# One rounding buffer, asked for once, for the second batch's four token blocks of a quantised GLU kernel

## The chip, the core and the metric

The kernel runs on one core of one Trainium2 chip. The core has five engines that run side by side, each with its own instruction queue that it works off in order: TensorE (PE, with its weight loads shown apart as PEld), VectorE (DVE), ScalarE (ACT), GpSimd (POOL) and SyncE (SP), which issues nearly all of this kernel's DMA transfers. The metric is the time of one execution on the device in microseconds (us), as the median of several runs.

## The reference

For each of four batches, 1024 tokens of width 512 are normalised, scaled by a gain that comes from a condition vector, multiplied by an up-projection of 4096 rows, gated, rounded to 8 bits per token, and multiplied by a down-projection whose weights are rounded to -1, 0 or 1:

```python
scale = cond @ norm_w.T + 1.0
ms = jnp.mean(x * x, axis=-1, keepdims=True)
h = x * (scale[:, None, :] * jax.lax.rsqrt(ms + EPS))
u = h @ up_w.T
val, gate = jnp.split(u, 2, axis=-1)
h = val * jax.nn.gelu(gate, approximate=False)
hq = act_quant(h)          # per token: round(h * 127 / max|h|), scaled back
wq = weight_quant(down_w)  # round(w / mean|w|) in -1, 0, 1, scaled back
return hq @ wq.T + x
```

## The kernel before

**Arithmetic.** The up-projection needs more digits than one f16 number holds, so each f32 operand is kept as two f16 numbers, a high part (the value rounded to f16) and a low part (the rest). One product of a 256-wide piece then takes six matmuls: high by low, low by high and high by high, for two blocks of 128 (`TERMS`). Weights and tokens are both cut into two halves, and the four block products of a 2x2 block multiplication are made from seven (`C_ALL = 7`), with sums and differences of the halves as operands.

**Stages.** Batch b has 16 slots, one for each block of 128 hidden columns; slot g = 16b + j makes the gate and the value of block j for all 1024 tokens of the batch. The first batch is made in another way while the weights are still being prepared: its blocks 0 to 11 by plain products (`half_gate`, `half_value`), its blocks 12 to 15 by slots. The order of everything in this stage is written out by hand in a long string, `FIRST_BATCH`, in which each word is a step: `slot.14.5` is the sixth step of slot 14, `t_high.3.2` is step `high` of token block 3, part 2. Each engine takes its steps in the order of the string. The steps of a slot have numbers: 0 is the first product, 1 its copy into bank B, 2 the fourth product (its copy is 3), 4 the fifth product, which adds to the first one's bank, 5 its copy to t2 (line 820), 6 the second product, 8 the third, 10 the gate product, 13 the value product, which adds to the bank that step 5 has copied.

**The second batch's tokens.** In the same stage the tokens of batch 1 are made ready, in four blocks a = 0 to 3 of 2 x 128 tokens (class `Tokens`). For each block: load; square and root; scale by the gain; four sums of halves; then `high` (ACT casts f32 to f16, line 665), `low` (DVE subtracts, line 669) and `turn` (SP issues a DMA transpose into the big tile `R`, line 673). These last three come in three parts: part 0 is operands 0 and 1 (written `nx[:, 0:2]`), part 1 is operand 2 (`nx[:, 2:3]`), part 2 is operands 3 to 6 (`nx[:, 3:7]`). The tile `nx` that holds the high and low parts before the transpose is the rounding buffer of this document. It is asked for by `place` from a pool with one buffer (`tag="nx", bufs=1`). A tile asked for from such a pool may be written first when every access to the tile before it in that place is over, whatever region that access touched.

**The order around block 3.** Blocks 2 and 3 follow each other in the buffer. SP turns block 2 as part 2, part 0, part 1. Between part 0 and part 1 stand, in SP's queue, a weight transpose, two transposes of the last weight rows and spills, and the first load of a piece of the down-projection (`d_fetch`, line 546). On ACT the casts `t_high.3.2` and `t_high.3.0` stand ahead of `slot.14.3`, a small gain, and `slot.14.5`. After them ACT casts the last weight rows of block 15 (`s_high.15.1`, line 453), POOL subtracts (`s_low.15.1`, line 457), and SP turns them (`s_turn.15.1`, line 475), followed by block 3's part 0 and part 2. Slots 14 and 15 and then batch 1's slots 16, 17 and on are what PE has next. SP's transfers use eight completion semaphores, DMAHW0 to DMAHW7, one after the other; each transfer waits for the one that used its semaphore last.

Of the kernel before, what the change touches and what calls it, by code (L numbers as in the profile page):

```python
# [51 lines left out]
def glu_quant_kernel(  # L52
# [108 lines left out]
    def h_slots(g, n=1):  # L161
        s = g % NSLOT
        return H[:, s : s + n]
# [414 lines left out]
    class Tokens:  # L578
# [69 lines left out]
            ]  # L648

        def place(self):  # L650
            if self.nx_at is None:
                self.nx = wpool.tile(
                    [P, C_ALL, 2, HALF], F16, name=f"nx_{self.b}_{self.a}", tag="nx", bufs=1
                )
            else:
                v = h_slots(self.nx_at, 2).bitcast(F16).rearrange("p s h t -> p (s h t)")
                self.nx = v[:, : C_ALL * 2 * HALF].rearrange(
                    "p (c l d) -> p c l d", c=C_ALL, l=2
                )
# [366 lines left out]
    class Pair:  # L1026
# [12 lines left out]
        def sum1(self, place):  # L1039
            self.s[1] = place.bitcast(BF16)  # L1040
            DVE.tensor_tensor(self.s[1], self.part(1, 0), self.part(1, 1), ALU.add)
# [237 lines left out]
    toks, ams, made = {}, {}, {}  # L1279
# [247 lines left out]
    for b in range(1, B):  # L1527
# [23 lines left out]
        if b + 1 < B:  # L1551
            sc = []
            steps[3, "z"] = [(lambda b=b, sc=sc: sc.append(cond_load_scale(b + 1)), (0, 0))]
            steps[5, "z"] = [(lambda b=b, sc=sc: cond_bring(b + 1, sc[0]), (0.4, 0))]
            p0 = b * NJ + 12
            plan = [
                (None, p0, ((6, "z"), (7, "x"), (7, "y"), (9, "y"), (10, "x"), (10, "z"))),
                (p0 + 4, None, ((9, "y"), (10, "x"), (10, "y"), (11, "y"), (12, "x"), (12, "x"))),
                (None, None, ((10, "y"), (11, "x"), (11, "y"), (13, "x"), (13, "y"), (13, "z"))),
                (p0 + 2, p0 + 4, ((9, "z"), (12, "x"), (12, "y"), (14, "x"), (14, "y"), (14, "z"))),  # L1560
            ]
            for a, (at, nx_at, places) in enumerate(plan):
                def make(a=a, at=at, nx_at=nx_at, b=b):
                    toks[a] = Tokens(b + 1, a, at, nx_at)
                    toks[a].load()
                fs = [
                    make,
                    lambda a=a: toks[a].norm(),
                    lambda a=a, sc=sc: toks[a].scale_and_sum(sc[0]),
                    lambda a=a: toks[a].high(),  # L1570
                    lambda a=a: toks[a].low(DVE),
                    lambda a=a: toks[a].turn(),
                ]
                costs = ((0, 0), (0, 1.6), (0, 1.5), (0, 2.1), (2.6, 0), (0, 0))
                for place, f, c in zip(places, fs, costs):
                    steps.setdefault(place, []).append((f, c))
# [250 lines left out]
```

## Time and profile before

| | |
|---|---|
| Median of 3 runs | 728.83 us (728.76 to 731.47) |
| The profiled execution's own time | 728.52 us |
| Its span, first to last instruction | 726.4 us |
| PE busy | 714.6 us, 98% of the span |
| DVE busy | 589.7 us, 81% |
| ACT busy | 423.0 us, 58% |
| POOL busy | 135.7 us, 19% |
| Granted TensorE clock, mean | 0.995 of full speed |

The span is 2.1 us less than the time of the same execution. Slots and products can be followed in the rows of line 698 (seven-product scheme, six matmuls each) and line 713 (plain). In the profile, a row of a timeline gives the start in us from the span's start, the duration, engine, line, operation and tiles, how often, and in brackets how long the engine stood idle ahead of it and what ended that. SPq is SP's sequencer, so the duration there is the issue of a transfer, not the transfer. A row of waits reads: engine, tile and line that waited, what it waited for, total us, times, longest us. Of overlapping instructions on one engine each has its own start, so a row's start plus duration may lie a little past the next row's start.

### The profile page before, as it was taken

How to read it: one execution, taken by the hardware profiler on the slowest of the kernel's cores; microseconds unless marked ns; L12 is line 12 of the kernel's file. 1: busy time of each engine (PE TensorE's matmuls, PEld its weight loads, DVE VectorE, ACT ScalarE, POOL GpSimd, SP SyncE). 2: the span in 40 equal slices, each digit the busy share in tenths (PEclk: the TensorE clock that was granted, in tenths of full speed). 3: DMA queues.
4: the chain of work that ended last, by engine and by line, in shares of the span. 5: the costliest groups of instructions: out<-in, count | busy, mean ns of one | idle time of the engine just before them, and what ended most of it. 6: DMA issues, size and time to landing. Idle time of an engine off the chain costs nothing.

```text
span 726.4 us, 10223 instructions
## 1 busy us (share of the span) xinstructions
PE 714.6 (98%) x3664; PEld 360.1 (50%) x3664; DVE 589.7 (81%) x880; ACT 423.0 (58%) x703; POOL 135.7 (19%) x143
## 2 busy tenths in 40 slices
PE   8999999996999999999999999999999999999998
PEld 4544444442444446665444445666444444445854
DVE  7898898885898879898688877877679888765896
ACT  6998777664757775544335676544433665333463
POOL 1712323240100033540010030360020000000120
PEclk9999999998999999999999999999999999999999
DMA  6899899997886644976745546865955444444243
GB/s 221 282 268 297 236 232 261 251 214 171 218 197 153 153 110 159 193 184 163 172 102 117 131 101 175 197 153 153 218 103 109 102 103 102 100 93 109 103 156 134
DMA packets 227060, 121.57 MB, mean 167 GB/s; under 512 B 188969, under 2 KB 198461, under 8 KB 227010
## 3 DMA queue, kind: packets, MB, share of 16 engines
q1 hardware_dynamic: 226858, 120.80, 66.6%
q8 instruction: 28, 0.46, 0.3%
q14 instruction: 22, 0.18, 0.1%
q10 hardware_dynamic: 152, 0.13, 0.1%
HBM read 52.71 MB, written 23.09 MB: 104 GB/s over the span
## 4 chain that ended last, share of the span: by engine, by line
PE 96%; ACT 1%; DMA 1%; DVE 1%; issue 0%; SPq 0%; POOL 0%; ACTq 0%
PE A L698 36%; PE E L698 18%; PE po L1062 9%; PE B L698 9%; PE pg L713 8%; PE pv L713 8%; PE po_end L1014 4%; PE pz L1179 1%; DMA R<-nx 1%; PE ptx L1163 1%; DMA R<-s_rows 0%; PE pv L784 0%; PE po_B L1062 0%; PE pg L784 0%; PE pw L382 0%
## 5 line engine op out<-in xcount | busy, mean ns | idle before, releaser
L698 PEld LDWEIGHTS <-SXY 128*128 128x128 f16 x2100 | 205.6, 98 | 241.0 <-issue 0.8
L698 PE MATMUL A<-R,SXY 128*128 128x512 f16 x1146 | 265.1, 379 | 0.0
L698 PE MATMUL E<-R,SXY 128*128 128x512 f16 x582 | 141.4, 379 | 0.0
L833 DVE SCALAR_TENSOR_TENSOR H<-A,sg,t 128x512 f32<-128x512 f32 x52 | 39.0, 750 | 67.5 <-PE A L698 67.3
L985 DVE TENSOR_TENSOR H<-H,am 128x1024 f32<-128x1024 f32 x64 | 76.0, 1213 | 0.0
L844 ACT ACTIVATE t<-t,sg 128x512 f32<-128x512 f32 x52 | 37.5, 720 | 62.8 <-DVE t L841 62.6
L698 PE MATMUL B<-R,SXY 128*128 128x512 f16 x300 | 72.9, 379 | 0.0
L904 DVE TENSOR_REDUCE gm<-H 128x512 f32<-128x1024 f32 x56 | 69.0, 1232 | 1.0
L827 ACT ACTIVATE t<-B,sg 128x512 f32<-128x512 f32 x52 | 35.7, 687 | 37.6 <-PE B L698 37.5
L920 POOL PARTITION_ALL_REDUCE am<-R x8 | 14.3, 1793 | 231.4 <-DVE R L906 231.4
L713 PEld LDWEIGHTS <-SXY 128*128 128x128 f16 x342 | 33.4, 98 | 40.3 <-DVE SXY L424 0.4
L1062 PE MATMUL po<-wd,R 128*128 128x256 fp8e4 x416 | 52.4, 273 | 0.0
L820 ACT COPY t<-A 128x512 f32<-128x512 f32 x52 | 30.2, 580 | 37.9 <-PE A L698 37.5
L813 ACT COPY v<-E 128x512 f32<-128x512 f32 x52 | 30.4, 585 | 31.8 <-PE E L698 31.4
L1062 PEld LDWEIGHTS <-R 128*128 128x128 bf16 (+1 forms) x448 | 43.8, 98 | 8.9
L805 ACT COPY B<-A 128x512 f32<-128x512 f32 x52 | 29.7, 572 | 31.6 <-PE A L698 30.8
L853 DVE SCALAR_TENSOR_TENSOR H<-v,sg,t 128x512 f32<-128x512 f32 x52 | 41.0, 789 | 7.1 <-ACT t L844 7.1
L850 DVE TENSOR_TENSOR v<-A,v 128x512 f32<-128x512 f32 x52 | 35.6, 685 | 10.3 <-PE A L698 8.7
L993 ACT ACTIVATE H<-H 128x1024 f32<-128x1024 f32 x38 | 39.9, 1050 | 5.2 <-DVE H L985 5.2
L713 PE MATMUL pg<-R,SXY 128*128 128x512 f16 x180 | 41.3, 379 | 0.0
L906 DVE TENSOR_TENSOR R<-R,gm 128x512 f32<-128x512 f32 x56 | 40.1, 716 | 1.1
L997 ACT ACTIVATE R<-H 128x1024 bf16<-128x1024 f32 x38 | 40.1, 1056 | 1.0
(237 smaller groups left out, 951.1 us busy)
## 6 DMA issues: line engine op xcount, KB each, us to landing
SXY<-s_dram SPq DMA_DIRECT2D x46, 256.0 KB, 3.2
H<-in_L_cond_up_w_dram SPq DMA_DIRECT2D x13, 512.0 KB, 4.8
SXY<-s_dram SPq DMA_DIRECT2D x46, 128.0 KB, 3.3
s_dram<-SXY SPq DMA_DIRECT2D x15, 384.0 KB, 5.1
xr<-in_x_dram SPq DMA_DIRECT2D x19, 256.0 KB, 2.9
out_dram<-xr SPq DMA_DIRECT2D x19, 256.0 KB, 2.5
H<-in_x_dram SPq DMA_DIRECT2D x8, 512.0 KB, 7.8
R<-in_L_cond_down_w_dram SPq DMA_DIRECT2D x8, 512.0 KB, 7.0
```

The lines of the kernel that those rows point to most:

```text
L698: PE.matmul(o, s[:, w, k, :], operand(g // NJ, c, l, k), start=start and n == 0, stop=stop and n == len(TERMS) - 1, skip_group_check=True,)
L713: PE.matmul(ps, a[k // 2][:, w, k % 2, :], XP[:, l, k, h * TOK : (h + 1) * TOK], start=n == 0, stop=n == len(terms) - 1,)
L827: ACT.activation(self.t1, self.B, AF.Gelu, scale=gain(self.g, 1))
L833: DVE.scalar_tensor_tensor(h_half(self.g, 0), self.A, gain(self.g, 0), self.t1, ALU.mult, ALU.mult)
L844: ACT.activation(self.t2, self.t2, AF.Gelu, scale=gain(self.g, 1))
L853: DVE.scalar_tensor_tensor(h_half(self.g, 1), self.v, gain(self.g, 0), self.t2, ALU.mult, ALU.mult)
L904: DVE.tensor_reduce(gm[0], v, AX.X, ALU.max, apply_absolute_value=True)
L906: return [largest, lambda: DVE.tensor_tensor(m, m, gm[0], ALU.max)]
L985: DVE.tensor_tensor(v, v, r.to_broadcast([P, 2, TOK]), ALU.mult)
L993: ACT.activation(v, v, AF.Copy, bias=MAGIC)
L997: ACT.activation(q, by_tile(v), AF.Copy, bias=-MAGIC)
L1062: PE.matmul(po, w[:, j], m, start=start and j == 0, stop=stop and j == n - 1, skip_group_check=True,)
```

## The change

```diff
         def place(self):
-            if self.nx_at is None:
+            if self.nx_at is None and self.b == 1 and self.a:
+                self.nx = toks[0].nx
+            elif self.nx_at is None:
                 self.nx = wpool.tile(
                     [P, C_ALL, 2, HALF], F16, name=f"nx_{self.b}_{self.a}", tag="nx", bufs=1
                 )
```

Block 0 of batch 1 asks for the buffer as before. Blocks 1, 2 and 3 of batch 1 take the same tile object. The bytes are the same bytes as before, since the pool had one buffer for this tag. What differs is what the framework waits for: a write to a region of a tile that is already held waits for the accesses to that region alone. Batches 2 and 3 are not touched.

No instruction is added, removed or moved: on PE, DVE, ACT, POOL and SP the instructions stand in the same order before and after (lines behind the edit are numbered 2 higher). What changes is the list of semaphores in front of eight casts on ACT and six subtractions on DVE that write the buffer. The place that the prediction speaks of is ACT's, at block 3. Before, ACT from the weight cast of block 15 to the copy of slot 14's fifth product:

```order
L805 COPY B_14_1661<-A_14_1654 128x512 [waits PE_49,Activation_49]
L453 CAST s_rows_15_0_1676<-H_79 128x2x256 [waits DMAHW2_49,DMAHW1_49,DVE_49]
L665 CAST nx_1_3_1683<-xt_1_3_1497 128x4x256 [waits DMAHW2_49,DMAHW0_49,DMAHW3_49,DVE_49,Pool_49]
L665 CAST nx_1_3_1683<-xa_1_3_1496 128x2x256
L813 COPY v_14_1702<-E_14_1666 128x512 [waits DVE_49,PE_49]
L360 ACTIVATE sg_0_104<-sw_103,dx_101 128x4
L820 COPY t2_14_1711<-A_14_1654 128x512 [waits PE_49,Activation_49]
```

The same place after the change:

```order
L807 COPY B_14_1659<-A_14_1652 128x512 [waits PE_49,Activation_49]
L453 CAST s_rows_15_0_1674<-H_79 128x2x256 [waits DMAHW2_49,DMAHW1_49,DVE_49]
L667 CAST nx_1_0_963<-xt_1_3_1495 128x4x256 [waits DMAHW0_49,DVE_49,Pool_49]
L667 CAST nx_1_0_963<-xa_1_3_1494 128x2x256 [waits DMAHW3_49]
L815 COPY v_14_1699<-E_14_1664 128x512 [waits DVE_49,PE_49]
L360 ACTIVATE sg_0_104<-sw_103,dx_101 128x4
L822 COPY t2_14_1708<-A_14_1652 128x512 [waits PE_49,Activation_49]
```

The first cast of block 3 waited for DMAHW0, DMAHW3 and DMAHW2, that is for all three transposes of block 2; now it waits for DMAHW0 alone, which is part 2's transpose, and the second cast waits for DMAHW3, part 0's. The wait for DMAHW2, part 1's, moves to the cast of part 1, some fifteen instructions further on in ACT's queue. The value of the DVE semaphore that the first cast waits for also falls by one, from the last subtraction of block 2 to the last sum of block 3.

SP's transfers from block 2's first transpose on, before the change (the same afterwards but for names); a row that waits for a DMAHW semaphore is also the one that raises it next, and the first row raises DMAHW0:

```order
L673 DMA_TRANSPOSE R<-nx_2_1425 128x16x128 [waits DVE_49]
L475 DMA_TRANSPOSE R<-s_rows_0_1592 128x8x128 [waits DMAHW1_49,DVE_49]
L469 DMA s_dram<-s_rows_0_1592 128x1024 [waits DMAHW2_49]
L673 DMA_TRANSPOSE R<-nx_2_1425 128x8x128 [waits DMAHW3_49]
L406 DMA_TRANSPOSE SXY<-H 128x12x128 [waits DMAHW4_49,DVE_49,PE_49]
L475 DMA_TRANSPOSE R<-s_rows_1_1593 128x8x128 [waits DMAHW5_49,DVE_49]
L469 DMA s_dram<-s_rows_1_1593 128x1024 [waits DMAHW6_49]
L469 DMA s_dram<-s_rows_0_1676 128x1024 [waits DMAHW7_49,Pool_49]
L475 DMA_TRANSPOSE SXY<-s_rows_0_1676 128x8x128 [waits DMAHW0_49]
L546 DMA dn_1713<-in_L_cond_down_w_dram 128x1024 [waits DMAHW1_49,DVE_49]
L673 DMA_TRANSPOSE R<-nx_2_1425 128x4x128 [waits DMAHW2_49]
L546 DMA dn_1725<-in_L_cond_down_w_dram 128x1024 [waits DMAHW3_49,DVE_49]
```

Part 1's transpose (the row of 4x128) stands ten transfers behind part 2's and seven behind part 0's. Blocks 1 and 2 get the same kind of edit on their casts: block 1's first cast no longer waits for part 1 of block 0, and block 2's first cast waits for part 0 of block 1 where it waited for all three parts.

## Prediction

> **What bounds the kernel now.** I read the page first, then the waits of the first 240 us, then the chain and the timelines around the one long wait.
>
> ```profile
> PE   8999999996999999999999999999999999999998
> ```
>
> The row is PE's busy share in 40 slices of 18.2 us. PE is full almost everywhere, so time can be won only where PE stands still: one slice, the tenth (163 to 182 us), shows a 6, and behind it come thirty full ones. Whatever PE loses in the tenth slice, the whole rest of the kernel starts later by that much.
>
> ```profile
> ACT nx L665 <- DMA R<-nx: 8.3, 1, 8.3
> DVE nx L669 <- ACT nx L665: 7.5, 1, 7.5
> PE A L698 <- ACT t L820: 5.8, 1, 5.8
> ```
>
> These three single waits are one event. ACT stands 8.3 us in front of a cast into the rounding buffer, until a transpose out of that buffer has landed; DVE then waits for the cast; and PE waits 5.8 us for a copy that stands behind the cast in ACT's queue. The chain that ended last goes through it:
>
> ```profile
> 164.88 4.49 DMA R<-nx
> ...
> 169.55 0.07 ACT nx L665
> ```
>
> The transpose issued at 164.88 landed at 169.37. On PE it looks like this:
>
> ```profile
> 163.75 1.46 PE L698 MATMUL A<-wd,R 128*128 128x512 f16 x6
> 165.04 1.46 PE L698 MATMUL E<-R,SXY 128*128 128x512 f16 x6
> 172.32 2.72 PE L698 MATMUL A<-wd,R 128*128 128x512 f16 x6 [5.82 <-ACT t L820]
> 174.84 1.75 PE L698 MATMUL A<-R,SXY 128*128 128x512 f16 x6
> 176.42 1.46 PE L698 MATMUL E<-wd,SXY 128*128 128x512 f16 x6
> ...
> 184.19 1.46 PE L698 MATMUL A<-R 128*128 128x512 f16 x6
> 185.49 1.46 PE L698 MATMUL E<-R 128*128 128x512 f16 x6
> ```
>
> A product of six matmuls comes every 1.295 us (163.75 to 165.04). Without a wait the value product of slot 14 would start at 166.34 and the one that stands at 176.42 at 165.04 + 3 x 1.295 = 168.93. It comes 7.49 us late. Of that, 172.32 - 166.34 = 5.98 us are standstill, and 1.51 us are two products that ran slowly after it. The granted clock (the number ahead of the DMA share) says why:
>
> ```profile
> 166.00:168.00 2.00, 0.50 (x3) 0.11 (x2) 0.00 (x0) 0.00 (x0) 0.00 (x0) 1.00 0.92 234
> 168.00:170.00 2.00, 0.00 (x0) 0.00 (x0) 0.00 (x0) 0.45 (x1) 0.00 (x0) 0.65 0.40 77
> 170.00:172.00 2.00, 0.00 (x0) 0.00 (x0) 1.37 (x2) 2.00 (x5) 0.00 (x0) 0.50 0.01 4
> 172.00:174.00 2.00, 1.68 (x5) 0.57 (x5) 2.00 (x5) 0.84 (x2) 1.08 (x1) 0.50 0.41 125
> 174.00:176.00 2.00, 2.00 (x8) 0.80 (x7) 1.51 (x4) 1.30 (x2) 0.07 (x1) 0.65 0.73 208
> ```
>
> It falls to 0.50 during the standstill and stays there for the first products after it.
>
> **The change, part by part.** Nothing is added, removed or moved; only waits differ. Blocks 1 and 2 first: their casts lose waits too, but of the whole line 665 the table of waits has one entry, the 8.3 us above. A wait that cost nothing gives nothing back: 0.
>
> Block 3's first cast. It waited for all of block 2's transposes, and the last of them, part 1, is the one issued at 164.88. Now it needs part 2's transpose, DVE's and POOL's sums, and ACT free.
>
> ```profile
> 160.64 0.62 ACT L453 CAST s_rows<-H 128x512 f16<-128x512 f32 x1
> 169.55 1.04 ACT L665 CAST nx<-xt 128x1024 f16<-128x1024 f32 x1 [8.29 <-DMA R<-nx]
> 170.50 0.61 ACT L665 CAST nx<-xa 128x512 f16<-128x512 f32 x1
> 171.02 0.58 ACT L813 COPY v<-E 128x512 f32<-128x512 f32 x1
> 171.70 0.57 ACT L820 COPY t<-A 128x512 f32<-128x512 f32 x1
> 172.22 0.62 ACT L453 CAST s_rows<-H 128x512 f16<-128x512 f32 x1
> ```
>
> ```profile
> 160.53 0.41 DVE L634 TENSOR_TENSOR xt<-xa 128x256 f32<-128x256 f32 x1
> 162.36 0.73 DVE L853 SCALAR_TENSOR_TENSOR H<-v,sg,t 128x512 f32<-128x512 f32 x1
> 170.63 1.23 DVE L669 TENSOR_TENSOR nx<-xt,nx 128x1024 f16<-128x1024 f32 x1 [7.54 <-ACT nx L665]
> ...
> 172.71 0.74 DVE L833 SCALAR_TENSOR_TENSOR H<-A,sg,t 128x512 f32<-128x512 f32 x1
> ```
>
> ```profile
> 158.07 0.72 POOL L634 TENSOR_TENSOR xt<-xa,xt 128x256 f32<-128x256 f32 x1
> 172.92 1.15 POOL L457 TENSOR_TENSOR s_rows<-H,s_rows 128x512 f16<-128x512 f32 x1 [10.42 <-ACT s_rows L453]
> ```
>
> ```profile
> 150.05 2.54 SPq L673 DMA_TRANSPOSE R<-nx  x1
> 156.64 1.29 SPq L673 DMA_TRANSPOSE R<-nx  x1
> 164.88 1.20 SPq L673 DMA_TRANSPOSE R<-nx  x1
> 171.88 0.34 SPq L546 DMA_DIRECT2D dn<-in_L_cond_down_w_dram  x1
> 174.10 1.24 SPq L475 DMA_TRANSPOSE SXY<-s_rows  x1
> 175.43 1.30 SPq L673 DMA_TRANSPOSE R<-nx  x1
> 177.40 1.68 SPq L673 DMA_TRANSPOSE R<-nx  x1
> ```
>
> ```profile
> DMA to landing us min/median/max: 5.2/5.8/7.0
> dn<-in_L_cond_down_w_dram SPq DMA_DIRECT2D x3, 512.0 KB, 4.5
> ```
>
> The first three SP rows are block 2's parts 2, 0 and 1; the last two are block 3's parts 0 and 2; the last fence has the landing times of line 673's transposes, as far as the profile gives them, and of the down-projection loads. Step by step:
>
> - The cast of part 2: POOL's sums end at 158.79, DVE's at 160.94, the transpose at 150.05 + 7.0 = 157.05 at the latest, ACT's cast before it at 161.26. It starts at 161.3, not 169.55, and ends at 162.3.
> - The cast of part 0: its transpose has landed by 156.64 + 7.0 = 163.64 at the latest, so it ends between 162.9 and 164.25.
> - The copy of v needs DVE's row of 162.36, which ends at 163.09: over by 164.83 at the latest, the small gain by 165.1.
> - The copy t (line 820) needs slot 14's fifth product, whose row ends at 163.75 + 1.46 = 165.21. It then takes 0.57 us: 165.8. PE wants it at 166.34. The standstill is gone with 0.5 us to spare, and with it the slow clock.
>
> So PE is 7.49 us earlier from the slot 15 products on. The other engines are free when that is asked of them: DVE's subtractions of block 3 come right after 163.1, or after the second cast, instead of at 170.63. From there to the end of the read that frees slot 13's bank are 173.45 - 170.63 = 2.82 us, which puts that end near 166 us, ahead of 167.63, when slot 15's first product wants the bank.
>
> What is late next is the queue of SP, which gains less than PE. The load at 171.88 stood 6.1 us for DVE's subtraction; that is now over at about 164.3, so the load goes out when SP is free, 164.88 + 1.20 = 166.1: 5.8 us earlier. The weight transpose at 174.10 waits for POOL, POOL for ACT's cast at 172.22, and that cast now follows the t copy at 165.8: ACT ends at 166.4, POOL 1.15 us later at 167.6, so 6.5 us earlier. Block 3's transposes follow at 168.9 and 170.9. Batch 1's first product needs part 0 at 184.19 - 7.49 = 176.7, its fourth needs part 2 at 178.0. With the longest landing seen they are there at 175.9 and 177.9. Both hold, the second by 0.1 us at the worst landing and by 1.3 us at the median. From there on PE drives SP and DVE, and all move together to the end.
>
> Sum: 728.52 us of the profiled execution - 7.49 = 721.0. The median of the runs is 0.31 us above that execution, which gives 721.3 us. The most the wait itself could return is ACT's 8.3 us, hence 720.5 as the edge below; I take 720.3 with the spread of the runs.
>
> **The rivals.**
>
> *A, the transfers take a part back.* The three transposes and the 512 KB load come 5.8 to 6.5 us earlier, into DMA engines that were 0.92 busy at 166 to 168 and drained only by 170 (0.40, then 0.01). If that backlog must be gone first, the group can start at 169.37 rather than 171.88 and moves by 2.5 us alone. Part 2 of block 3 then lands at 177.40 + 5.8 - 2.5 = 180.7, at worst 181.9, and PE waits 2.7 to 3.9 us for it at 178.0. The gain shrinks to between 4.8 and 3.6 us: 724.0 to 725.2. Against it speaks that the backlog is thin: of the stretch from 168 to 170 it fills 0.40.
> The Trainium skill, "DMA: Bandwidth & Descriptors", section "Queues, rings and completion order", speaks for A: on each DMA engine descriptors are consumed in the order of the ring, and SP owns one ring per engine, so the load that now goes out earlier stands ahead of the transposes that PE needs. By that rule alone the sum would be A's 724.0 to 725.2, if the ring is still full; the row at 168 to 170 says it is 0.40 busy by then, so it bites for part of the way only.
>
> *B, nothing comes of it.* Another wait on ACT stands as late as the one removed, and t is copied at about 171.8 as before: 728.8. For it: a wait for several things is put down to the last, and others may hide behind it. Against it: each of the others is worked out above, and the latest is at 163.64.
>
> *C, slower.* Block 3's part 2 lands so late that PE stands longer than it does now, and the clock falls again. That needs a landing after 185.49, the time at which the fourth product of slot 16 starts today, 14.6 us after its new issue at 170.9, against 7.0 in the longest row. At 2 us beyond that point: 730.8.
>
> **How the numbers follow.** My own case (gain 6 to 8.3 us, 720.3 to 722.8) gets 0.73, since each step of it rests on a row and only the transfers lack one; A gets 0.13, B 0.06, C 0.08 for everything that I don't see. About half a per cent, 3.6 us, is what a measurement of this kernel can tell from no change, so faster means below 725.2: 0.73 + 0.12 of A = 0.85. B and the rest of A make 0.07 for the same, C 0.08 for slower. The range is my case and the nearer part of A: 720.3 to 724.8.
>
> **What would show it.** In the profile after: no row of the cast line waiting on R<-nx for over 1 us; the cast at about 161.3 and t's copy at 165.3; PE's value product at 166.3 with no bracket behind it; a granted clock of 1.00 from 160 to 180; the digit 6 of the tenth slice a 9. If A holds, a new wait of PE stands near 178 us with R<-nx as its releaser. I am wrong if slot 14's value product still waits for the copy of t, or if PE stands still anywhere between 170 and 200 us.

## The result and the profile after

Over eight runs of each kernel on one chip the median falls from 729.37 us (728.34 to 731.47) to 724.18 us (721.33 to 726.84). The ratio is 0.9927 with a 95% interval of 0.9903 to 0.9951. On two other chips the same changed kernel had medians of 721.32 us (ratio 0.9901, 0.9888 to 0.9914) and 721.71 us (0.9911, 0.9895 to 0.9927). The three intervals overlap, and together they reach from a gain of 0.5% to one of 1.1%.

The profiled execution of the changed kernel took 722.66 us, with a span of 720.8 us and a mean granted clock of 1.000 (before 728.52, 726.4 and 0.995). Lines behind the edit are numbered 2 higher: 698 is now 700, 665 is 667, 673 is 675, 820 is 822, 805 is 807. This profile also starts its middle part 0.35 us earlier than that of before (slot 14's fourth product at 164.69 instead of 165.04), so a time read from it is compared with the prediction after adding 0.35.

The row of PE's busy share over 40 slices:

```profile
PE   8999999999899999999999999999999999999998
```

The 6 of the tenth slice is a 9. An 8 stands in the eleventh, 180 to 198 us. The table of waits for the stretch from 100 to 260 us, cut to the rows that matter (engine, tile and line, what was waited for, total us, times, longest):

```profile
ACT dn L550 <- issue: 3.5, 1, 3.5
...
PE B L700 <- ACT B L807: 1.7, 1, 1.7
...
PE A L700 <- ACT t L822: 0.2, 1, 0.2
```

The wait of the cast for R<-nx, 8.3 us before, is not in the table any more, and PE's wait for the copy t has gone from 5.8 to 0.2 us (that 0.2 is at another slot, 184.5 us). In their place stand two others: ACT stands 3.5 us at line 550, where it stood 1.15 us before, and PE 1.7 us for a copy of line 807, a wait that the profile of before does not have. First the place of the edit. ACT's timeline at block 3:

```profile
160.29 0.62 ACT L453 CAST s_rows<-H 128x512 f16<-128x512 f32 x1
160.82 1.04 ACT L667 CAST nx<-xt 128x1024 f16<-128x1024 f32 x1
161.76 0.61 ACT L667 CAST nx<-xa 128x512 f16<-128x512 f32 x1
162.83 0.59 ACT L815 COPY v<-E 128x512 f32<-128x512 f32 x1 [0.45 <-DVE H L855]
...
164.95 0.59 ACT L822 COPY t<-A 128x512 f32<-128x512 f32 x1 [1.34 <-PE A L700]
```

The first cast follows the weight cast without a gap. The copy t no longer stands behind the cast; it waits for PE, whose fifth product it reads. PE's timeline there, and where the new wait is:

```profile
163.40 1.46 PE L700 MATMUL A<-wd,R 128*128 128x512 f16 x6
164.69 1.46 PE L700 MATMUL E<-R,SXY 128*128 128x512 f16 x6
165.99 1.46 PE L700 MATMUL A<-wd,R 128*128 128x512 f16 x6
167.28 1.46 PE L700 MATMUL A<-R,SXY 128*128 128x512 f16 x6
168.58 1.46 PE L700 MATMUL E<-wd,SXY 128*128 128x512 f16 x6
...
187.12 1.46 PE L700 MATMUL E<-R,SXY 128*128 128x512 f16 x6
190.28 1.46 PE L700 MATMUL B<-R,SXY 128*128 128x512 f16 x6 [1.71 <-ACT B L807]
```

From 163.40 to 168.58 a product comes every 1.295 us with no bracket. At 190.28 the second product of slot 17 comes 190.28 - 187.12 - 1.295 = 1.87 us late. The chain that ended last, between 160 and 192 us, tells where that is from (an "issue" row is idle time for which the profile names no releaser):

```profile
177.67 5.54 DMA R<-nx
...
184.48 3.51 issue
187.99 1.15 ACT dn L550
189.14 0.61 ACT t L846
189.75 0.49 ACT B L807
...
190.28 1.46 PE B L700 x6
```

SP's timeline gives the transfers (for SPq the duration is that of the issue). The row L675 at 177.67 turns part 1 of block 3; the next one is the load of the down-projection's piece 3:

```profile
175.54 0.44 SPq L546 DMA_DIRECT2D H<-in_L_cond_down_w_dram  x1
177.67 1.29 SPq L675 DMA_TRANSPOSE R<-nx  x1
183.22 0.34 SPq L546 DMA_DIRECT2D dn<-in_L_cond_down_w_dram  x1
```

And the same three rows of the kernel before:

```profile
180.42 0.45 SPq L546 DMA_DIRECT2D H<-in_L_cond_down_w_dram  x1
185.51 1.20 SPq L673 DMA_TRANSPOSE R<-nx  x1
187.96 0.34 SPq L546 DMA_DIRECT2D dn<-in_L_cond_down_w_dram  x1
```

Then ACT's rounding of piece 3 and its copy into bank B, and the product that reads the copy, all before the change:

```profile
192.91 1.15 ACT L550 ACTIVATE dn<-dn,wsc 128x1024 f32<-128x1024 f32 x1 [1.15 <-issue]
...
194.75 0.57 ACT L805 COPY B<-A 128x512 f32<-128x512 f32 x1
```

```profile
195.84 1.46 PE L698 MATMUL B<-R,SXY 128*128 128x512 f16 x6
```

and the same copy after it:

```profile
189.66 0.57 ACT L807 COPY B<-A 128x512 f32<-128x512 f32 x1
```

Piece 3 is loaded into the rounding buffer's place: in the code, `d_fetch(3)` asks for a tile with the same tag `nx`. So it waits for the transpose of block 3's part 1 to have read the old contents. With the 0.35 us taken off, that transpose is issued 7.49 us earlier than before, as much as PE gained. But the 512 KB load of piece 2 ahead of it (the rows of 180.42 and 175.54) comes only 4.5 us earlier, so the transpose now stands 2.1 us behind that load and not 5.1. The load of piece 3 goes out 5.55 us after the transpose's issue instead of 2.45, and so gains 4.4 us and not 7.5. It is on ACT's queue that this is felt: line 550 rounds piece 3, and behind it stands the copy into bank B that PE's second product waits for. The profile names no releaser for ACT's wait there. That it is the load is read from the code and from the times: ACT begins 4.8 us after the load's issue, and began 4.95 us after it before.

### The profile page after: what moved, and what is told of

The parts are those of the page before. It is cut to its first block, busy times and chain, and to the rows that moved or that the text cites. A ratio compares the mean times of both kernels' runs of the same rounds, so it can differ in the third digit from the quotient of the medians.

```text
span 720.8 us, 10222 instructions
## 1 busy us (share of the span) xinstructions
PE 712.9 (99%) x3664; PEld 359.6 (50%) x3664; DVE 589.5 (82%) x880; ACT 423.2 (59%) x703; POOL 134.7 (19%) x143
## 4 chain that ended last, share of the span: by engine, by line
PE 97%; DMA 1%; ACT 1%; issue 1%; DVE 0%; SPq 0%; DVEq 0%
PE A L700 36%; PE E L700 18%; PE po L1064 9%; PE B L700 9%; PE pg L715 8%; PE pv L715 8%; PE po_end L1016 4%; DMA R<-nx 1%; PE pz L1181 1%; PE ptx L1165 1%; PE pv L786 0%; PE po_B L1064 0%; PE pg L786 0%; PE pw L382 0%; PE po_A L1064 0%
```

## The experiments

The kernels ran in three groups, each on a chip of its own, and each is compared with runs of the kernel before on the same chip. Those had medians of 728.37 us (first four rows), 729.19 us (next four) and 728.49 us (last two).

| run | median us (range) | ratio to before, 95% interval |
|---|---|---|
| block 3 alone | 722.80 (721.49 to 725.05) | 0.9922 (0.9907 to 0.9938) |
| blocks 1 and 2 alone | 728.76 (727.91 to 729.36) | 1.0001 (0.9992 to 1.0010) |
| the change again | 721.32 (720.30 to 722.52) | 0.9901 (0.9888 to 0.9914) |
| part 1 earlier | 720.45 (720.22 to 721.51) | 0.9891 (0.9878 to 0.9904) |
| turn earlier, no shared tile | 722.44 (721.19 to 722.86) | 0.9912 (0.9898 to 0.9925) |
| PE kept busy in the wait | 727.65 (726.86 to 730.52) | 0.9981 (0.9972 to 0.9990) |
| rounding of piece 3 later | 721.25 (720.58 to 721.84) | 0.9898 (0.9884 to 0.9911) |
| small load of piece 2 | 720.71 (719.89 to 720.79) | 0.9888 (0.9875 to 0.9902) |
| the change, third chip | 721.71 (721.26 to 724.73) | 0.9911 (0.9895 to 0.9927) |
| part 1 earlier, third chip | 720.75 (720.48 to 721.01) | 0.9889 (0.9874 to 0.9904) |

### Which block holds the gain

Block 3 alone takes block 2's tile; blocks 1 and 2 ask for their own as before:

```diff
-            if self.nx_at is None:
+            if self.nx_at is None and self.b == 1 and self.a == 3:
+                self.nx = toks[2].nx
+            elif self.nx_at is None:
```

> Only block 3 takes the held buffer (block 2's); blocks 1 and 2 ask for a new one as before. My theory (all of the gain is the 8.3 us wait of block 3's first cast): the same as the full change, 721 to 725 us, no wait of ACT on R<-nx over 1 us, PE's standstill of 5.8 us gone, the granted clock 1.00 from 160 to 180 us. Rival (the gain needs the looser waits of blocks 1 and 2 as well): between 725 and 729 us, with part of the 8.3 us wait left.

The other half, in which block 3 asks for its own:

```diff
-            if self.nx_at is None:
+            if self.nx_at is None and self.b == 1 and self.a in (1, 2):
+                self.nx = toks[0].nx
+            elif self.nx_at is None:
```

> Blocks 1 and 2 take block 0's buffer; block 3 asks for a new one. My theory: as the kernel before, 728.3 to 730 us, with ACT's wait of about 8.3 us on R<-nx and PE's 5.8 us standstill. Rival (blocks 1 and 2 carry part of the gain): below 727 us.

Block 3 alone gave 722.80 us, blocks 1 and 2 alone 728.76 us against 728.37 us of before. The waits of the second run, 100 to 260 us, still hold the old event:

```profile
ACT nx L667 <- DMA R<-nx: 8.1, 1, 8.1
...
PE A L700 <- ACT t L822: 5.6, 1, 5.6
```

So the gain is block 3's, and the waits of blocks 1 and 2 cost nothing, as worked out. Block 3 alone shows the new wait too, and longer, 4.7 us on ACT and 2.8 us on PE. That is 1.1 us more on PE than with the whole change, whose median on the same chip is 1.5 us lower (next section); the two intervals overlap.

### The change again

> The changed kernel once more, on the chip of the other three, since its eight runs went from 721.3 to 726.8 us. My theory (the scatter comes from the new wait: ACT for the down-projection load that stands behind block 3's part 1 in the buffer, 3.5 us on ACT and 1.7 us on PE in the profile of after): PE's wait is again there, between 0.5 and 5 us, and the time is 721 plus about that wait. Rival (the scatter is the chip's, as of any kernel): the kernel before scatters as widely beside it.

It gave 721.32 us, and the same new waits in its profile: 3.5 us on ACT at line 550 and 1.7 us on PE. Its four runs lie within 2.2 us and the seventeen of the kernel before beside it within 1.8 us, so on this chip alone the spread does not tell the two apart.

### The new wait taken away by order

Part 1's cast, subtraction and transpose stand earlier in the written order, so that the transpose is issued ahead of piece 2's load. Nothing else differs from the changed kernel:

```diff
-        slot.13.11 slot.13.12 max.4.0.1 slot.15.0 slot.14.7 slot.14.14 slot.15.1 max.5.0.0 t_turn.3.0
-        slot.15.2 slot.13.15 slot.15.3 s_spill.11.2 slot.15.6 max.5.0.1 t_turn.3.2 max.4.1.0 slot.14.8
+        slot.13.11 slot.13.12 max.4.0.1 slot.15.0 slot.14.7 slot.14.14 slot.15.1 t_high.3.1 max.5.0.0 t_turn.3.0
+        slot.15.2 slot.13.15 t_low.3.1 slot.15.3 s_spill.11.2 slot.15.6 max.5.0.1 t_turn.3.2 t_turn.3.1 max.4.1.0 slot.14.8
...
-        t_high.3.1 slot.14.12 slot.15.14 d_sign.1 t_low.3.1 t_turn.3.1 slot.14.15 max.6.0.0 d_fetch.3
+        slot.14.12 slot.15.14 d_sign.1 slot.14.15 max.6.0.0 d_fetch.3
```

> The change, and block 3's part 1 (cast, subtraction, transpose) moved ahead by about 6 us: the cast behind slot 15's first copy, the transpose right behind part 2's. Thereby the buffer is free, and the down-projection load that reuses it goes out, about 4 us earlier. My theory (the 1.9 us that are missing from the forecast 7.5 are this load's wait): no wait of PE over 0.5 us from 160 to 240 us, time 720.0 to 721.5 us, and little scatter. Rival (the transfers as a whole are too slow once the standstill is gone): the wait shows up again at another transfer, and the time stays at 722 to 725 us.

It gave 720.45 us, 7.9 us below before. SP's timeline (the two transposes of block 3's parts 2 and 1 share a row):

```profile
171.81 3.68 SPq L675 DMA_TRANSPOSE R<-nx  x2
...
177.71 0.44 SPq L546 DMA_DIRECT2D dn<-in_L_cond_down_w_dram  x1
```

Piece 3's load goes out at 177.71, 5.5 us earlier than in the changed kernel, and PE's products run through the place of the new wait:

```profile
186.90 1.46 PE L700 MATMUL E<-R,SXY 128*128 128x512 f16 x6
188.19 1.46 PE L700 MATMUL B<-R,SXY 128*128 128x512 f16 x6
```

The interval of this run overlaps that of the change again, so the times alone do not prove the 0.9 us between their medians; the two profiled executions differ by 722.52 - 720.57 = 1.95 us, and the 1.87 us at the second product are gone.

### The wait shortened without the shared tile

The kernel before, with block 2's last transpose moved up on SP, ahead of two transfers of weight rows and the first load. No tile is shared, so block 3's cast still waits for it, only for less long:

```diff
-        s_high.15.0 s_low.15.0 t_low.2.1 max.4.0.0 t_high.3.2 slot.14.6 t_high.3.0 slot.12.15 s_spill.15.0
+        s_high.15.0 s_low.15.0 t_low.2.1 t_turn.2.1 max.4.0.0 t_high.3.2 slot.14.6 t_high.3.0 slot.12.15 s_spill.15.0
...
-        t_turn.2.1 t_low.3.0 slot.13.10 slot.13.9 d_fetch.1 s_high.15.1 s_low.15.1 s_turn.15.1 slot.14.13
+        t_low.3.0 slot.13.10 slot.13.9 d_fetch.1 s_high.15.1 s_low.15.1 s_turn.15.1 slot.14.13
```

> The kernel before, every block with a new buffer as before, but the transpose of block 2's part 1 moved ahead of three transfers in SP's queue (a spill, a weight transpose, a down-projection load), so that it can go out about 3.4 us earlier, at 161.5 instead of 164.9. My theory (that transpose's landing is what ACT's cast waits for, and PE loses what ACT waits plus the slow clock): it lands near 166, ACT waits 4 to 5.5 us instead of 8.3, PE stands 2 to 3 us instead of 5.8, the clock stays at 1.00, and the time is 723.5 to 725.5 us. Rival (the wait has another releaser behind it): ACT waits over 7 us, time 728 to 729.5 us.

It gave 722.44 us. Its chain, then ACT's and PE's timelines:

```profile
161.83 2.45 DMA R<-nx
```

```profile
164.38 1.04 ACT L665 CAST nx<-xt 128x1024 f16<-128x1024 f32 x1 [2.88 <-DMA R<-nx]
```

```profile
167.15 1.46 PE L698 MATMUL A<-wd,R 128*128 128x512 f16 x6 [0.42 <-ACT t L820]
```

The transpose was issued 3.05 us earlier and landed after 2.45 instead of 4.49 us, so the cast came 5.2 us earlier, and PE's standstill of 5.82 us shrank to 0.42 us. A wait of 2.9 us on ACT costs PE next to nothing, one of 8.3 us costs it 5.8 us: the cause lies in when the cast may begin, however that is brought about. The gain was larger than expected: the wait was forecast with a landing near 166 us, and it came at 164.28. The transpose stands ahead of three transfers that it stood behind before; that this is why it landed sooner was not tried by itself. This kernel has the late load of piece 3 as well, with 2.8 us of waiting on ACT at line 550 and 0.9 us on PE, although it shares no tile.

### The slow clock by itself

The kernel before, with 24 matmuls at the place of the standstill, on data at hand and into a bank that nobody reads. They are extra work; all of the kernel's own stays:

```diff
+    def hot_steps(n):
+        pz = po_bank("pz_hot")
+        for i in range(n):
+            PE.matmul(pz, XP[:, 0, 0, :P], XP[:, 0, 0, :TOK], start=True, stop=True)
...
-        t_turn.2.1 t_low.3.0 slot.13.10 slot.13.9 d_fetch.1 s_high.15.1 s_low.15.1 s_turn.15.1 slot.14.13
+        t_turn.2.1 t_low.3.0 slot.13.10 hot.24 slot.13.9 d_fetch.1 s_high.15.1 s_low.15.1 s_turn.15.1 slot.14.13
```

> The kernel before with 24 further matmuls of 128x512 on data that lies in SBUF, written to a bank that nobody reads, between slot 13's gate product and slot 14's value product, that is inside PE's standstill of 5.8 us: they take 24 x 0.216 = 5.2 us. My theory (1.5 us of the 7.5 are the clock that fell in the standstill): the granted clock stays at 1.00, the two products behind it run in 1.3 us each, and the time falls by about 1.5 us, 726.5 to 727.5 us. Rival (the two products are slow for another reason, such as DMA or bank traffic): no change, 728 to 729 us.

It gave 727.65 us, 729.19 - 727.65 = 1.5 us below the kernel before on its chip (the interval of the ratio makes that 0.7 to 2.0 us). PE's timeline and one of the windows (2 us each; the granted clock is the number ahead of the DMA share):

```profile
166.00 5.34 PE L1316 MATMUL pz_hot<-R 128*128 128x512 f16 x24
171.95 1.45 PE L698 MATMUL A<-wd,R 128*128 128x512 f16 x6 [0.60 <-ACT t L820]
173.24 1.46 PE L698 MATMUL A<-R,SXY 128*128 128x512 f16 x6
174.53 1.46 PE L698 MATMUL E<-wd,SXY 128*128 128x512 f16 x6
```

```profile
170.00:172.00 2.00, 1.40 (x8) 0.54 (x6) 1.75 (x3) 2.00 (x6) 0.00 (x0) 1.00 0.01 4
```

The value product comes 5.95 us after 166.00, when PE would have wanted it, close to the 5.98 us of before, but at full clock, and the two behind it follow at 1.29 us. The third of these products stands 174.53 - 166.00 = 8.53 us behind the time at which PE was free, and 176.42 - 166.34 = 10.08 us before. So the 1.51 us put down to the slow clock are there as a cost of their own, and of about that size. The median bears it out less firmly: it lies 0.15 us above the range expected, and the profiled execution, the longest of its eleven, also carries a new wait near 194 us (last section), which the others may have in part.

### The new wait taken away in two other ways

Piece 3 is rounded one place later in ACT's list of the next stage, everything else as in the changed kernel:

```diff
-        ((0, "x"), d_round, 2), ((0, "x"), d_sign, 2), ((0, "y"), d_round, 3),
+        ((0, "x"), d_round, 2), ((0, "x"), d_sign, 2), ((1, "x"), d_round, 3),
```

> The change, and ACT's rounding of the down-projection piece that lies in the shared buffer moved back in ACT's queue by four instructions, behind slot 17's gate activation, some 6 us later. The load itself stays where it is. My theory (PE's 1.7 us are ACT standing in front of the rounding with the copy into B behind it): ACT's wait is gone or below 0.5 us, no wait of PE over 0.5 us between 160 and 240 us, time 720 to 721.5 us. Rival (SP's own standstill for the buffer, 4.2 us, delays the weights of slot 18 as well): PE waits for the weights instead, time 722 us or more.

And piece 2's load, the one ahead of the transpose, cut to an eighth:

```diff
-        SP.dma_start(out=v, in_=down_w[c * P : (c + 1) * P, u * HF : (u + 1) * HF])
+        w = HF // 8 if n == 2 else HF
+        SP.dma_start(out=v[:, :w], in_=down_w[c * P : (c + 1) * P, u * HF : u * HF + w])
```

> The change, with the load of down-projection piece 2, the 512 KB that stand in SP's queue ahead of block 3's part 1, cut to its first 64 KB; the other seven eighths of that piece are left out of the result. My theory (part 1's transpose lands 5.5 us after its issue instead of 2.4 because the transfers ahead of it are no longer done when it is issued): it lands 2.4 to 4 us after its issue, ACT's wait falls from 3.5 us to below 2, PE's from 1.7 to below 0.4, time 720 to 721.5 us. Rival (a transpose takes 5.5 us there whatever stands ahead): the waits stay at 3.5 and 1.7 us, time 721 to 723 us.

The later rounding gave 721.25 us and a profile in which PE has no wait between 100 and 260 us. The small load gave 720.71 us, also without a wait of PE. SP's timeline of the latter:

```profile
178.08 1.20 SPq L676 DMA_TRANSPOSE R<-nx  x1
180.52 0.34 SPq L547 DMA_DIRECT2D dn<-in_L_cond_down_w_dram  x1
```

With an eighth of the load ahead of it, the transpose lets piece 3's load go after 2.44 us, as in the kernel before, instead of 5.55. It stands 3.1 us behind that load; where it stands 3.4 to 3.6 us behind the whole 512 KB, the same step takes 3.7 to 5.5 us (last section). So the 512 KB ahead of the transpose are what makes it late. The medians of these two runs cannot be told from the change's on the other chips, since the intervals overlap; what they show is in the profiles.

### What spreads the runs of the change

In the first comparison the eight runs of the change spread over 5.5 us and those of the kernel before over 3.1 us. The change's last four are all above 725 us and carry mean granted clocks of 0.995 to 0.998; the other four have 0.999 to 1.000. The pair on a third chip asks whether the spread is the chip's.

> The changed kernel, unaltered, once more, beside e10. Its own runs so far lie between 720.3 and 726.8 us, and the ones above 725 were never profiled. If the late load of the third down-projection piece is what spreads them, ACT stands in front of its rounding (line 550) for 3 us or more in the profile, PE's copy wait on B is above 1 us, and the longer runs carry a granted clock below 0.999, as in the run with matmuls in the wait, where 2.0 us of standstill near 194 us were followed by a clock of 0.58. The median is then 721 to 725 us and the scatter over 1.5 us. If the spread belongs to the chip and not to this load, e10 scatters as much as this one.

> The changed kernel with block 3's part 1 moved ahead of the second down-projection piece in the written order, as in e4, on whatever chip this is. If the late load is the cause of the spread, PE has no wait near 188 us, all runs lie within 1.5 us of each other at 720 to 721.5 us, and the median is 0.5 to 4 us below e9's. If the spread is the chip's, both kernels scatter alike.

The change gave 721.26 to 724.73 us, part 1 earlier 720.48 to 721.01 us, with 0.8 us of waiting left on ACT at line 550 and none of PE for the copy into bank B. On the two chips where both ran, part 1 earlier had eight runs within 1.3 us (720.22 to 721.51) and the change nine within 4.4 us (720.30 to 724.73). So on these two chips the spread goes with the late load. On the first chip, where it was widest, part 1 earlier was not run. The longest run carries a mean clock of 0.998, its four companions 1.000; the profiled one shows 1.7 us of PE standing, and the longest was not the profiled one. That a longer standstill with a slow clock behind it makes the long runs fits, and the section on the hardware has an execution of another kernel in which just that happened, but no long run of the changed kernel itself was seen in a profile.

## Why the prediction was right, and where it was wrong

The time lies inside the range and on the predicted side; the median of 724.18 us is 2.9 us above the 721.3 us predicted. It is not inside the prediction's own case (720.3 to 722.8 us) but where rival A put it (724.0 to 725.2 us), and the range holds it because the nearer part of A had been taken in. A's wait is not what put it there, so that part is luck. The profiled execution (722.66 us) and the medians on the other two chips (721.32 and 721.71 us) do lie in the own case.

- **Blocks 1 and 2: 0.** Measured 1.0001 (0.9992 to 1.0010). Right.
- **Block 3's steps.** With the 0.35 us added: first cast 161.2 (predicted 161.3), second cast over at 162.7 (162.9 to 164.25), copy t from 165.3 to 165.9 (165.2 to 165.8), value product 166.34 (166.34), first product of batch 1 at 176.70 (176.7). Right within 0.2 us, and the value product runs without a wait, with 0.45 us to spare where 0.5 was predicted.
- **Standstill 5.98 us and slow clock 1.51 us.** Both gone, the second measured apart. Where the new wait is taken away, before and after differ by 728.37 - 720.45 = 7.9 us (the interval makes that 7.0 to 8.9), against 7.49 us worked out.
- **SP's queue up to block 3's transposes.** The first load at 166.17 (166.1), the weight transpose at 167.66 (167.6), part 0's at 169.0 (168.9). Part 2's came at 172.8 and not at 170.9, since the issue before it took 3.15 us instead of 1.30. The fourth product of slot 16 still started on time, at 177.64 + 0.35 = 177.99 (178.0), so that transpose had landed within 5.2 us. With the median of 5.8 us that the prediction used, PE would have stood 0.6 us: this step came out right, but not by its own sum.
- **"From there on PE drives SP and DVE, and all move together to the end."** This is the step that failed. Part 1's transpose and the load of piece 3 were not priced. With the 0.35 us taken off throughout, the transpose did move with PE, by 7.49 us, but SP's load of piece 2 ahead of it gained only 4.5 us. The transpose then took 3.1 us longer, and the load that wants its buffer gained 4.4 us. The copy into bank B, behind that piece's rounding on ACT, gained 194.75 - 189.66 - 0.35 = 4.74 us, which is 2.75 us behind PE. Before, the copy was over 0.5 us ahead of its product (195.32 against 195.84), and that was all the spare time there was.

In the profiled execution the second product of slot 17 is 195.84 - 190.28 - 0.35 = 5.21 us earlier than before and not 7.49: 2.28 us are lost. Of these, 1.87 us stand at that product and 0.41 us a little earlier, at 184.53, of which 0.25 us stand as a wait. The span of before, 726.4 us, less 7.49 and less the 0.35 us by which this execution was ahead at block 3 already, plus 2.28, gives 720.84 us; 720.8 were measured. From span to time it is 1.9 us here and 2.1 before. On the chip of the comparison the runs above 725 us add the rest of the distance to 724.18 us, and what PE waited for in those is not shown.

Rival A had the kind right and the place wrong. The transfers did take a part back, 2.3 us in the profile where A had 2.7 to 3.9, but not by PE waiting for block 3's part 2 near 178 us. It was part 1, which PE does not wait for there at all, that held back the next user of its buffer. B and C did not happen. By its own sign, PE standing anywhere between 170 and 200 us, the prediction was wrong in this part: PE stood 0.25 us ahead of 184.53 and 1.71 us ahead of 190.28.

## What to carry to other kernels

A tile that is asked for anew from a pool with one buffer waits until every access to its predecessor is over, whatever region that touched; a tile that is held on to waits region by region, and here that was worth 7.5 us to PE without an instruction added or moved, of which the profile shows 2.3 us given back at the buffer's next user. When a wait is removed, list everything that next asks for the same buffer and for the same queue, and carry the saving through to each, since a transfer that is issued earlier is issued into another neighbourhood and takes another time to land. Take the landing time from a row with the same transfers ahead of it, not from the median of its line. Here the line's landings were given as 5.2 to 7.0 us, while block 2's part 1 took 4.49 and block 3's 2.45 in the same profile.

## What the runs showed of the hardware that was not expected

**One transpose, 2.4 to 6.2 us.** Block 3's part 1 is the same 4x128 transpose in every kernel; with part 1 earlier it shares a row with part 2 and is left out here. From its issue to the issue of the load that waits for it passed 2.45 us in the kernel before, 2.44 us with blocks 1 and 2 alone and with the small load, 3.67 us with the later rounding, 4.33 us with the turn earlier, 5.2 to 5.55 us in three profiles of the change, 5.52 us with the matmuls in the wait, and 6.21 us with block 3 alone. In all those above 3 us it was issued 2.1 to 3.6 us behind the 512 KB load of piece 2; in the first two 5.1 and 5.85 us behind it, and with the small load 3.1 us behind 64 KB. The load itself took 6.1 us to land in the profile of the change. The distance alone does not order them: 3.4 to 3.6 us behind the load the step took 3.67, 4.33 and 5.52 us, and 2.1 us behind it 5.55. The Trainium skill, "DMA: Bandwidth & Descriptors", section "Queues, rings and completion order", has descriptors consumed in ring order on each DMA engine. The runs agree as far as they go: what was issued shortly before, and how much of it, makes the transpose late.

**The clock fell after 2.0 us of standing.** In the profiled execution of the kernel with matmuls in the wait, which took 730.52 us and was the longest of its eleven, the late load of piece 3 appears as well, and PE stands 2.0 us near 194 us. PE's timeline and two windows there:

```profile
196.11 2.56 PE L698 MATMUL B<-R,SXY 128*128 128x512 f16 x6 [1.99 <-ACT B L805]
```

```profile
194.00:196.00 2.00, 0.12 (x1) 0.00 (x0) 0.39 (x1) 2.00 (x3) 0.00 (x0) 1.00 1.26 360
196.00:198.00 2.00, 1.89 (x5) 0.70 (x5) 1.93 (x3) 0.65 (x2) 0.00 (x0) 0.58 1.06 232
```

The granted clock drops to 0.58 behind it and a product takes 2.56 us, while the change's 1.7 us and the 2.8 us of block 3 alone are followed by a clock of 1.00 in every 2 us window up to 200 us. The Trainium skill, "TensorE: Matmul & The Clock Gate", section "Part 1: The HAM clock gate (the "warmup" mystery)", names one idle window of about 3.4 us as the condition, on a window that runs freely. The 5.8 us of the kernel before agree with that. The 2.0 us do not, since they hold no such idle window, and the 2.8 us that kept the clock show that the length of the standstill alone does not decide. The drop behind 2.0 us was seen in one execution, and its cause stays open.
